# Attention followed by a clustering block: where one running maximum, the evictions and three scores stand in the order of the work

## The chip, the core and the metric

The kernel runs on one core of one Trainium2 chip. The metric is the time of one execution on the device in microseconds (us), as a median over several runs. Beside it there is one profiled execution, from which every row below comes.

The engines are named as in the profile: PE is TensorE (matrix products; PEld is its weight load), DVE is VectorE, ACT is ScalarE, POOL is GpSimd, SP is SyncE, which here only issues DMAs. Each engine works through its own queue in order. Matrix products are written to PSUM; the kernel's three PSUM pools together hold eight banks of 512 float32 per partition.

## What is computed

The input x is (4, 256, 64, 64) in float32, four images of N = 4096 points with C = 256 channels. Layer 0 is attention over the points of an image, layer 1 a block of clustering, a two-layer perceptron and a pointwise convolution. Cut to what matters:

```
# layer 0, per image; xf is (256, 4096)
q = wq @ xf + bq                # 32 x 4096
k = wk @ xf + bk                # 32 x 4096
v = wv @ xf + bv                # 256 x 4096
attn = softmax(q.T @ k, over the keys)
x = gamma * (v @ attn.T) + x
# layer 1
y = x + ls1 * cluster(group_norm(x))              # four cluster centres per head and fold
y = y + ls2 * (w2 @ gelu(w1 @ group_norm(y) + b1) + b2)    # 256 -> 1024 -> 256
z = relu(batch_norm(y * dw_w))
out = relu(batch_norm(wpw @ z))
```

## The kernel before, in words

**Stages.** The images follow one another. For each there is attention (`weighting`), then the clustering (`cluster`), then the perceptron and the last convolution (`mlp`, "multilayer part" below). The order of all instructions is written out by hand. Work of the next image is put between: `fill(n)` issues its projections of k, q and v one by one, and `mlp` issues its first scores.

**Units.** In attention the 4096 queries are cut into 8 blocks of 512 (`nb`) and the 4096 keys into 8 groups of 512 (`g`). A unit u = 8 nb + g is one group for one block, so an image has 64 units. A unit's scores are made in two halves of 256 keys (`half(u, h)`): two products into one PSUM tile of two banks (`products`, L423), a copy of it to SBUF on ScalarE (`kept`, L436) and a running maximum over the keys on VectorE (`highest_of`, L447). When all 16 halves of a block are done, `fold` (L504) joins the two rows of maxima; `highest` then reduces over the partitions with transposes (L534 to L551), writes the row to DRAM and reads it back to all partitions; the copy `known` (L569) puts it into `hold`. For block 1 of each image, where there is no time for that route, `across` and `spread` do it with PE.

**Who is ahead of whom.** Scores are made up to 11 units ahead (`LEAD`), so while block nb is weighed, the scores of block nb + 1 are made, by a table `at[u, part]`. Some halves have `kept_only`: their maximum is not taken from the PSUM tile but later, from the copy in SBUF. Such maxima are put on a list, `held`, and `caught(1)` takes one from it. The same is done for the second half of a block's first group (`g == 0`), of which the first half is only remembered (`saved`).

**What a unit does.** `exps(u + 1)` subtracts the block's maximum (two subtractions on VectorE, L586) and takes exponentials on ScalarE (L590 to L592), one quarter of them into the second half of `hold`. `factors(u + 1)` makes the sums of quarters that a product of two by two quarters with seven multiplications needs: one on VectorE (L609, it reads `hold`) and up to five on POOL (L595). `weigh(u, av, part)` (L661) multiplies with the values and adds up in four PSUM banks, `av` 0 to 3, in the order of `ORDER`, for the last unit of an image that of `LAST`. After the last group of a block `evict` (L686, ScalarE) takes the banks out, and `combine` joins them.

**Buffers.** The pool `ps_s` has two tiles of two banks. Within attention `hold` lives in one of them, so that one remains for scores. `ps_a` and `ps_m` have two banks each and hold `av`. In SBUF 13 tiles of one pool, `spool`, hold the image, the next image's input, the kept scores (`slots`), and what the multilayer part works on.

**Multilayer part.** It has 8 blocks of 512 points (7 in the third image, whose last is done later), in each four steps j. At the table's places `at[nb, j]` it makes a whole unit's scores of the next image (`score`), whose maxima go to a list `maxima` that `rest()` takes from one at a time (L495). `nxt.sums` are 32 sums of value quarters on POOL that the next image needs. Ahead of it stands the second group norm (`group_norm`, L277 to L297), for which the statistics of all points must be complete.

**The beginning** (`alone`) is the only place where the scores of an image's first block are not made beside another image's work.

Of the kernel before, what the change touches and what calls it, by code (L numbers as in the profile page):

```python
# [30 lines left out]
LEAD, SLOTS = 11, 10  # L31

QW = NB // 2
B21, B11, B12, B22 = range(4)
# [2 lines left out]


ORDER = (1, 5), (2, 3), (7, 6), (4,)
LAST = (7, 6), (1, 5), (2, 3), (4,)

PC = [
    "gn1_w", "gn1_b", "gn2_w", "gn2_b", "ls1", "proj_b", "ls2", "mlp_b2",
# [11 lines left out]
def attention_then_cluster_block(  # L57
# [250 lines left out]
    def attention(b, xs, ys):  # L308
# [146 lines left out]
        def half(u, h, kept_only=False):  # L455

            nb, g = divmod(u, GRP)
            if h == 0:  # L460
                begun(u)
            sc = products(u, h)
            kept(u, h, sc)
            own_copy = slots[u][:, PAIR[h]].rearrange("p h r n -> p r h n")
            if g == 0 and h == 0:
                highest_of(nb, own_copy)
            elif g == 0 or kept_only:
                held.append(lambda: highest_of(nb, own_copy))
            else:
                return lambda: highest_of(nb, tiles(sc))  # L470
            return lambda: None
# [328 lines left out]
        def alone():  # L800

            roots()
            for i in range(3):
                v_pair(i)
            staged("first", (("k", 0), ("q", 0)))
            k_unit(0)
            q_block(0)
            q_block(1)
            for i in range(3, 8):
                v_pair(i)  # L810
            for g in range(4):
                for f in sums(g):
                    f()
            for u in range(GRP):
                if u == 0:
                    begun(0)
                    staged("second", (("k", 1), ("q", 1)))
                    rest = load_rest()
                for h in range(2):
                    half(u, h)()  # L820
                caught(1)
                if u < 6:
                    v_pair(u + GRP)
                if u > 1:
                    next(rest, None)
            fold(0)
            for g in range(4, GRP - 1):
                for f in sums(g):
                    f()
            tp = turned_over(0, ps_m.tile([P, 4, P], F32, tag="m", name=f"tt_{b}_0"))  # L830
            half(GRP, 0)
            v_pair(14)
            dgs["dg"] = across(0, "w2", tp)
            spread(0, dgs["dg"])
            v_pair(15)
            wf()
            half(GRP, 1)
            exps(0)
            factors(0)
            for f in sums(GRP - 1):  # L840
                f()

# [31 lines left out]
        def weighting(next_x, fill, early, begin):  # L874
# [25 lines left out]
            for u in range(units):  # L900
# [35 lines left out]
                if u in shifts:  # L936
                    shift(shifts[u])
                weigh(u, av, 0)
                if g == GRP - 1:
                    evict(nb, av, 0 if more else 1)  # L940
                if short:
                    two = ps_s.tile([P, 2, NB], F32, tag="s", name=f"tt_{b}_{nb + 1}")
                    tp = turned_over(nb + 1, two[:, 0].rearrange("p (j n) -> p j n", j=4))
# [2 lines left out]
                weigh(u, av, 1)  # L946
                if short:
                    dgs["dg"] = across(nb + 1, "w2", tp)
                if g == GRP - 1:
                    evict(nb, av, 2 if more else 0)  # L950
                    if not more:
                        for _ in combine(nb, nc.vector):
                            pass
                if u == units - 2:
                    back_one(NBLK - 2)
                maxima = due(u, 2)
                if more and nb and g == GRP - 2:
                    known(mb)
                if g + 1 < GRP or more:
                    factors(u + 1)  # L960
                if ripe:
                    next(peak)
                    mb = next(peak)
# [81 lines left out]
    def cluster(b, ys, stats, cells, rest, fill, gelu, nxt, maxima, turn):  # L1045
# [342 lines left out]
        nxt.q_block(0)  # L1388
        nxt.k_unit(0)
        fill(1)  # L1390
        copies = []
        nxt.score(0, copies, maxima)
        copies.pop()()
        return stats2


# [116 lines left out]
    def mlp(b, ys, stats2, fill, nxt, blocks, turned, maxima):  # L1513
# [307 lines left out]
        acc, todo, slots = None, iter(()), (0,) * 4  # L1821
        own = ahead = iter(())

        at = {(u, 3): u for u in range(1, 7)} | {(7, 2): 7}
        if blocks < NBLK:
            at |= {(6, 1): 6, (6, 2): 7}
            del at[6, 3]
        for nb in range(blocks):
            end = nb == blocks - 1
            for j in range(4):  # L1830
                if j > 1:
                    rest()
                if end and j == 3:

                    rest()
                    rest()
                pw = (lambda: last(nb - 1, True, nc.gpsimd)) if end and j == 2 else lambda: None
                hs = first(nb, j, todo, slots, pw)
                if nb == 0 and j == 0:
                    fill(N)  # L1840
                if j > 1 or end:
                    rest()
                if nxt and nb:
                    for _ in range(2 if j < 2 else 1):
                        if nxt.sums:
                            nxt.sums.pop(0)()
                if j == 0:
                    if nb:
                        rectify = finish(nb - 1, acc)
                    acc = [  # L1850
                        ps_a.tile([P, NB], F32, tag=f"a{c}", name=f"mo{c}_{b}_{nb}")
                        for c in range(KC)
                    ]
                    if not end:
                        acc += [
                            ps_m.tile([P, NB], F32, tag="m", name=f"mo{c}_{b}_{nb}")
                            for c in range(2, 4)
                        ]
                    elif nxt:

                        nc.sync.dma_start(
                            out=a21_s, in_=w2.rearrange("(k p) m -> p k m", p=P)[:, :h_n, P:]
                        )
                        nxt.q_block(1)
                elif j == 1:
                    assert not drips and not hooks
                    if nb:
                        rectify()
                    if not end:
                        ahead = norm(nb + 1, nc.gpsimd)  # L1870
                        if nb:
                            own = factors(nc.gpsimd, pairs[nb - 1][:, 1], pairs[nb - 1][:, 0])
                        else:
                            own = left_factors()
                elif j == 2 and nb and not end:
                    pointwise(nb - 1)
                scored = nxt and (nb, j) in at
                if scored:
                    copies = []
                    nxt.score(at[nb, j], copies, maxima)  # L1880
                    copies.pop()()
                if len(acc) == KC:
                    todo = second(nb, acc, hs, j)
                    slots = (2, 1, 0, 1) if scored else (0, 1, 1, 2)
                else:
                    todo = second_by_seven(nb, acc, hs, j, own, ahead)
                    slots = (0, 2, 2, 3)
                    if scored:
                        slots = (3, 1, 2, 1)
                    elif j == 2 and nb:  # L1890
                        slots = (3, 1, 0, 3)
# [22 lines left out]
            nxt.exps(0, lambda: less(pairs[blocks - 1], nc.vector))  # L1914
        last(blocks - 1, bool(nxt), nc.vector, bool(nxt))
        if nxt:
            nxt.half(GRP, 1)
            nxt.factors(0)
        if blocks < NBLK:
            return late_block(b, y, gab)  # L1920
# [117 lines left out]
```

## Time and profile before

| | us |
|---|---|
| Runs of the kernel: median of 3 | 3239.3 |
| lowest and highest | 3239.08 and 3241.08 |
| The profiled execution | 3239.87 |
| its span, first to last instruction | 3237.8 |

The span and the time of the same execution differ by 2.1 us, which lie around the instructions. The granted TensorE clock is 0.99 on average. The costliest groups of instructions that bear on what follows, from the profile's list (busy time, mean of one):

| group | engine | count | busy us | mean ns |
|---|---|---|---|---|
| L436 copy of a score half | ACT | 512 | 514.8 | 1011 |
| L586 subtraction | DVE | 512 | 598.6 | 1209 |
| L609 sum of quarters | DVE | 256 | 311.7 | 1218 |
| L423 score product | PE | 1024 | 394.4 | 470 |
| L592 exponential, the longest of three | ACT | 256 | 266.9 | 1042 |

How to read it: a row's idle time is that of its engine just before the instruction, with the instruction that ended it behind an arrow. In timelines the columns are start, duration, engine, line, operation, what is written and read, and the shape. The profile splits a float32 product into two matmul rows, so counts of rows are not counts of products.

### The profile page before, as it was taken

To read this page: it belongs to the slowest core of one execution; us is meant where nothing else is said; L and a number is where in the kernel's file an instruction comes from. 1 tells how busy PE (TensorE), PEld (TensorE's weight loads), DVE (VectorE), ACT (ScalarE), POOL (GpSimd) and SP (SyncE) were. 2 spreads that over 40 slices of the span, in tenths; PEclk is the share of its full clock that TensorE was granted. 3 is DMA by queue.
4 is the path that set the end of the run, shared out by engine and by line. 5 is a ranking of instruction groups with operands and counts; after the bars stand their busy time and mean duration, and the time that the engine had idled before them with its cause. 6 is when DMAs were issued, how large, how long until landed. Compare 5 with 4: busy or idle time off the path is not lost.

```text
span 3237.8 us, 41259 instructions
## 1 busy us (share of the span) xinstructions
PE 3068.9 (95%) x14210; PEld 2504.8 (77%) x14210; DVE 2502.2 (77%) x3569; ACT 1772.2 (55%) x2807; POOL 2323.0 (72%) x2223
## 2 busy tenths in 40 slices
PE   6999999999999999999999999999999999998999
PEld 4778887788678888778867888786877787875786
DVE  3888887667788888777778888777678888877665
ACT  4566654545556665444555666634556566654444
POOL 3888888378488888648748888855866888894563
PEclk9999999999999999999999999999999999999999
DMA  4122126100111122610011221341011112150000
GB/s 162 40 59 62 53 63 187 51 32 30 43 49 54 61 59 85 165 50 20 30 50 49 62 59 56 111 128 50 30 43 43 53 59 62 56 142 7 14 20 27
DMA packets 105873, 200.39 MB, mean 62 GB/s; under 512 B 14416, under 2 KB 30400, under 8 KB 104128
## 3 DMA queue, kind: packets, MB, share of 16 engines
q1 hardware_dynamic: 101856, 181.94, 17.8%
q0 software_dynamic: 2976, 14.70, 2.4%
q8 instruction: 113, 1.85, 0.2%
q10 hardware_dynamic: 832, 1.11, 0.1%
q14 instruction: 96, 0.79, 0.1%
HBM read 149.37 MB, written 48.34 MB: 61 GB/s over the span
## 4 chain that ended last, share of the span: by engine, by line
PE 54%; DVE 15%; POOL 13%; ACT 10%; issue 6%; DMA 2%; ACTq 0%; SPq 0%; POOLq 0%; DVEq 0%
PE av L661 16%; PE mo L1650 10%; PE hq L1733 5%; POOL acc L595 5%; DVE top L447 4%; DVE s L586 4%; PE sc L423 4%; PE hp L1733 3%; PE hr L1733 3%; POOL t L595 3%; PE fv L1224 3%; PE vp L378 3%; ACT s L436 2%; ACT s L592 2%; POOL s L595 2%
## 5 line engine op out<-in xcount | busy, mean ns | idle before, releaser
L436 ACT COPY s<-sc 128x1024 f32<-128x1024 f32 x512 | 514.8, 1011 | 470.3 <-PE sc L423 468.8
L586 DVE TENSOR_TENSOR s<-s,hold 128x1024 f32<-128x1024 f32 x512 | 598.6, 1209 | 8.3 <-PE hold L576 8.3
L595 POOL TENSOR_TENSOR s<-t,s 128x512 f32<-128x512 f32 x256 | 345.4, 1349 | 315.5 <-DVE t L609 243.4
L661 PE MATMUL av<-t,v 128*128 128x256 f32 x2048 | 532.0, 382 | 14.0 <-DVE t L609 12.6
L595 POOL TENSOR_TENSOR acc<-acc,t 128x512 f32<-128x512 f32 x416 | 541.9, 1323 | 0.0
L661 PE MATMUL av<-s,v 128*128 128x256 f32 x2048 | 530.5, 382 | 7.1 <-ACT t L686 5.0
L661 PE MATMUL av<-s,sum 128*128 128x256 f32 x2048 | 527.1, 380 | 9.8 <-POOL s L595 9.8
L609 DVE TENSOR_TENSOR t<-s,hold 128x1024 f32<-128x1024 f32 x256 | 311.7, 1218 | 217.3 <-ACT s L592 64.7
L423 PE MATMUL sc<-q,k 128*128 128x512 f32 x1024 | 394.4, 470 | 79.0 <-DVE top L447 61.2
L661 PEld LDWEIGHTS av<-t,v 128*128 128x128 f32 x2048 | 389.8, 191 | 77.4 <-DVE t L609 16.5
L661 PEld LDWEIGHTS av<-s,v 128*128 128x128 f32 x2048 | 390.2, 191 | 71.1 <-ACT t L686 6.5
L661 PEld LDWEIGHTS av<-s,sum 128*128 128x128 f32 x2048 | 389.0, 190 | 66.2 <-POOL s L595 13.4
L447 DVE TENSOR_TENSOR top<-sc,top 128x1024 f32<-128x1024 f32 x326 | 397.7, 1220 | 40.1 <-ACT s L436 36.7
L1688 ACT ACTIVATE hs<-hs,pv_s 128x256 f32<-128x256 f32 x496 | 233.7, 503 | 344.4 <-DVE hs L1724 343.9
L1650 PE MATMUL mo<-hs,w 128*128 128x256 f32 x1512 | 390.4, 382 | 0.0
L595 POOL TENSOR_TENSOR t<-s 128x512 f32<-128x512 f32 x256 | 332.7, 1300 | 47.0 <-PE av L661 33.7
L1650 PEld LDWEIGHTS mo<-hs,w 128*128 128x128 f32 x1512 | 281.0, 190 | 54.3 <-ACT hs L1688 6.2
L423 PEld LDWEIGHTS sc<-q,k 128*128 128x128 f32 x1024 | 175.9, 189 | 164.7 <-DVE top L447 109.4
L590 ACT ACTIVATE hold<-s 128x512 f32<-128x512 f32 x256 | 154.2, 602 | 266.1 <-DVE s L586 261.0
L592 ACT ACTIVATE s<-s 128x1024 f32<-128x1024 f32 x256 | 266.9, 1042 | 0.0
L661 PE MATMUL av<-t,sum 128*128 128x256 f32 x1024 | 262.5, 378 | 0.9 <-DVE t L609 0.9
L1724 DVE TENSOR_TENSOR hs<-hq,hs 128x256 f32<-128x256 f32 x496 | 198.6, 421 | 79.9 <-PE hq L1733 69.9
(296 smaller groups left out, 4881.2 us busy)
## 6 DMA issues: line engine op xcount, KB each, us to landing
k<-k SPq DMA_DIRECT2D x256, 256.0 KB, 2.7
x<-in_x SPq DMA_DIRECT2D x62, 512.0 KB, 6.9
out<-xn SPq DMA_DIRECT2D x62, 256.0 KB, 2.1
att<-t SPq DMA_DIRECT2D x56, 256.0 KB, 3.8
x<-att POOLq DMA_DIRECT2D x12, 1024.0 KB, 10.0
q<-q SPq DMA_DIRECT2D x32, 256.0 KB, 4.1
w<-in_w SPq DMA_DIRECT2D x8, 1024.0 KB, 11.6
rden<-row_rd SPq DMA_DIRECT2D x28, 256.0 KB, 3.7
```

The costliest lines, as they stand in the source:

```text
L423: nc.tensor.matmul(sc[:, r, :], k_s[:, (2 * h + r) * P : (2 * h + r + 1) * P], qs[u // GRP], start=True, stop=True,)
L436: nc.scalar.copy(slots[u][:, PAIR[h]].rearrange("p h r n -> p r h n"), tiles(sc))
L447: nc.vector.tensor_tensor(top, src, top if saved[nb] is None else saved[nb], ALU.max)
L586: nc.vector.tensor_tensor(sh, sh, mb.to_broadcast([P, 2, 2, QW]), ALU.subtract)
L592: nc.scalar.activation(s[:, PAIR[1]], s[:, PAIR[1]], AF.Exp)
L595: nc.gpsimd.tensor_tensor(out, x, y, op)
L609: nc.vector.tensor_tensor(t31[u], s[:, B11 : B22 + 1 : 2], b12.to_broadcast([P, 2, 2, QW]), ALU.add)
L661: nc.tensor.matmul(av[bank][:, half_ * QW : (half_ + 1) * QW], a[:, r], t[:, r], start=(g == 0 and r == 0 and i in (1, 7, 2, 4)), stop=(g ...
L1650: return nc.tensor.matmul(bank[:, half * HB : (half + 1) * HB], a[:, j], t, start=start, stop=stop)
L1688: nc.scalar.activation(src, src, AF.Gelu_apprx_tanh, bias=pvc("b1", P, j + 4 * (i > 1)))
L1724: nc.vector.tensor_tensor(dst, ps, term, ALU.add)
L1733: nc.tensor.matmul(out, w, x, start=True, stop=True)
```

## The change

The change has six parts.

1. The maximum of the second half of a block's first group is no longer put on `held`: unless `kept_only` is given, it is taken from the PSUM tile. The two calls of `half(GRP, 1)` outside `weighting` now give `kept_only`.
2. In the last unit of a block the evictions of banks 0 and 2 (in an image's last block 0 and 1) stand together behind the copy of the score half that `due(u, 2)` makes. `known` now follows `factors`. `LAST` begins with products 1 and 5.
3. Before the multilayer part three units of the next image are scored instead of one (`EARLY`); the table `at` there has no scores in blocks 1 and 4.
4. Sums of value quarters are taken one per step instead of two, two, one, one, and three per step in the last block.
5. In `alone` k and q of the second half of the points are projected by `halved` (a tile of `ps_m` each) instead of `staged` (one tile of `ps_s`).
6. In `alone` the first exponentials and sums stand ahead of three of four last value halves, of the score half (8, 1), and of `wf`.

```diff
+EARLY = 3
...
-LAST = (7, 6), (1, 5), (2, 3), (4,)
+LAST = (1, 5), (7, 6), (2, 3), (4,)
...
-            elif g == 0 or kept_only:
+            elif kept_only:
                 held.append(lambda: highest_of(nb, own_copy))
             else:
                 return lambda: highest_of(nb, tiles(sc))
...
-                    staged("second", (("k", 1), ("q", 1)))
+                    halved("k", 1)
+                    halved("q", 1)
                     rest = load_rest()
                 for h in range(2):
                     half(u, h)()
-                caught(1)
...
             half(GRP, 0)
-            v_pair(14)
+            v_half(28)
             dgs["dg"] = across(0, "w2", tp)
             spread(0, dgs["dg"])
-            v_pair(15)
-            wf()
-            half(GRP, 1)
             exps(0)
             factors(0)
+            v_half(29)
+            v_pair(15)
+            half(GRP, 1, True)
+            wf()
...
                 weigh(u, av, 0)
-                if g == GRP - 1:
-                    evict(nb, av, 0 if more else 1)
...
                 weigh(u, av, 1)
...
+                if u == units - 2:
+                    back_one(NBLK - 2)
+                maxima = due(u, 2)
                 if g == GRP - 1:
-                    evict(nb, av, 2 if more else 0)
+                    evict(nb, av, 0)
+                    evict(nb, av, 2 if more else 1)
                     if not more:
                         for _ in combine(nb, nc.vector):
                             pass
-                if u == units - 2:
-                    back_one(NBLK - 2)
-                maxima = due(u, 2)
+                if g + 1 < GRP or more:
+                    factors(u + 1)
                 if more and nb and g == GRP - 2:
                     known(mb)
-                if g + 1 < GRP or more:
-                    factors(u + 1)
...
-        copies = []
-        nxt.score(0, copies, maxima)
-        copies.pop()()
+        for u in range(EARLY):
+            copies = []
+            nxt.score(u, copies, maxima)
+            copies.pop()()
...
-        at = {(u, 3): u for u in range(1, 7)} | {(7, 2): 7}
+        at = {(2, 3): 3, (3, 3): 4, (5, 3): 5, (6, 3): 6, (7, 2): 7}
...
-                    for _ in range(2 if j < 2 else 1):
+                    for _ in range(3 if end else 1):
                         if nxt.sums:
                             nxt.sums.pop(0)()
...
-            nxt.half(GRP, 1)
+            nxt.half(GRP, 1, True)
```

## The prediction, made before the result was known

> **What bounds the kernel now.** I read the engines' shares first, then the waits of TensorE, then the timelines around the longest of them.
>
> ```profile
> PE 3068.9 (95%) x14210; PEld 2504.8 (77%) x14210; DVE 2502.2 (77%) x3569; ACT 1772.2 (55%) x2807; POOL 2323.0 (72%) x2223
> ...
> PE sc L423 <- DVE top L447: 61.2, 64, 3.1
> PE av L661 <- DVE t L609: 13.5, 11, 2.0
> PE gnm_gn L279 <- DVE mv_gn L277: 12.8, 3, 4.3
> ```
>
> TensorE is busy 3068.9 of 3237.8 us, and the change alters none of its matmuls: at most the idle 169 us can be won. The other three lines (the view of the waits: total, times, longest) shows that the largest share is a score product waiting for VectorE's running maximum. One block of the second image, in the timeline (start, duration, engine, line):
>
> ```profile
> 1051.52 2.08 DVE L447 TENSOR_TENSOR top<-s,top 128x1024 f32<-128x1024 f32 x1
> ...
> 1053.40 0.59 ACT L569 COPY hold<-mr 128x512 f32<-128x512 f32 x1
> ...
> 1054.09 1.22 DVE L609 TENSOR_TENSOR t<-s,hold 128x1024 f32<-128x1024 f32 x1 [0.49 <-ACT hold L569]
> 1055.23 1.22 DVE L447 TENSOR_TENSOR top<-sc,top 128x1024 f32<-128x1024 f32 x1
> ...
> 1056.50 0.72 PE L423 MATMUL sc<-q,k 128*128 128x512 f32 x2 [1.46 <-DVE top L447]
> ...
> 1060.81 1.24 ACT L686 ACTIVATE t<-av,pv_s 128x512 f32<-128x512 f32 x2
> 1061.94 1.00 ACT L436 COPY s<-sc 128x1024 f32<-128x1024 f32 x1
> 1062.98 1.22 DVE L447 TENSOR_TENSOR top<-sc,top 128x1024 f32<-128x1024 f32 x1 [0.77 <-ACT s L436]
> 1064.26 0.73 PE L423 MATMUL sc<-q,k 128*128 128x512 f32 x2 [0.53 <-DVE top L447]
> ```
>
> Only one score tile circulates, since `hold` keeps the other buffer of `ps_s`: product, copy (1.0), maximum (1.2), next product. Two places per block break the beat: in unit 6 the held maximum from SBUF (2.08) and the copy of the next block's maximum (`known`, L569) push back L609; in unit 7 two evictions (1.24) stand ahead of a copy.
>
> The start times of VectorE's first subtraction (L586) give the rhythm: 7.00 us in units 0 to 3, though TensorE alone would need 6.88 (3.83 + 3.05 between scores that do not wait). So **the loop VectorE subtraction, ScalarE exponentials, L609, maximum, subtraction sets the pace**, and TensorE follows. From the subtraction in unit 5 to that in the next block's unit 0 (1041.43 to 1064.12) it takes 6.63 + 8.31 + 7.76 = 22.70. Over the 20 blocks 1 to 5 these stretches sum to 460.9.
>
> **Blocks 1 to 5.** The maximum of the first key group's second half, of the block whose scores are being made, moves from unit 6 to the end of unit 5 and reads PSUM. Replay with this trace's durations: it runs 1048.06 to 1049.28, so unit 6's first product, due at 1047.72, waits until 1049.33, a new stall of 1.6. Subtractions 1049.2 to 1051.5 (before from 1048.06), maximum to 1052.7, exponentials (2.10) to 1053.75, L609 to 1055.0 without waiting for `known`, second maximum to 1056.3, next subtraction 1056.2 (before 1056.37). In unit 7 exponentials end 1060.75, the copy now runs 1061.0 to 1062.0 ahead of the evictions, maximum to 1063.3, subtraction 1063.2 (before 1064.12). That is 21.8; I take 22.0 (up to 22.1 if queueing costs 0.3). `known` now waits for L609, which ends 1055.0; behind it on ScalarE is the copy of 1057.3, so 0.6 fits. The evictions end near 1064.5; bank 0 is due after 1064.7, bank 2 later: free. Where the row's DMA landed late, `known` ended 12.5 to 14.2 after unit 5's subtraction, and the next user now comes at 14.8: covered. 20 x 22.0 = 440, plus 2 for two stretches that hold matmuls of 1.9 instead of 1.03 us: **460.9 - 442 = 19 gained** (17 to 23).
>
> A rule against this: the Trainium skill, "PSUM — Partial Sum Buffer", section on bank collisions, says that two engines may not even read the same bank quadrant together, so copy and maximum must follow each other. The row agrees (the maximum waits for ACT s L436, 0.77), and it means that the new maximum holds the only tile. By the rule alone each block loses the 1.6: 32 us. By the subtraction rows TensorE has 0.12 per unit to spare and the 1.46 + 0.53 it lost later go away, so the loop decides. In its favour: "SBUF — State Buffer", "Who interferes with whom": VectorE with two SBUF inputs blocks against GpSimd's reads.
>
> ```profile
> L447 DVE TENSOR_TENSOR top<-sc,top 128x1024 f32<-128x1024 f32 x326 | 397.7, 1220 | 40.1 <-ACT s L436 36.7
> L447 DVE TENSOR_TENSOR top<-s,top 128x1024 f32<-128x1024 f32 x80 | 133.7, 1671 | 1.6
> ```
>
> The mean 1671 mixes 1.2 and 2.1; in these blocks the trace has 2.08. By the mean I would save 0.45 each, by the instance 0.86; the instance is used.
>
> **Block 0.** The same maximum now fills 1.24 us in unit 6 that VectorE idled for `hold`; TensorE lost 0.37 after it. 4 x 0.4 = **1.6**.
>
> **Block 6** has no scores left. There L609 waited for `known`, itself behind a shift (L757):
>
> ```profile
> 1285.76 2.17 ACT L757 ACTIVATE x<-x,gbv 128x1024 f32<-128x1024 f32 x2
> ...
> 1287.84 0.57 ACT L569 COPY hold<-mr 128x512 f32<-128x512 f32 x1
> 1288.50 1.22 DVE L609 TENSOR_TENSOR t<-s,hold 128x1024 f32<-128x1024 f32 x1 [4.84 <-ACT hold L569]
> ```
>
> L609 could go at 1285.9, so TensorE's 1.99 at 1289.78 vanishes. But the subtraction still needs `known` (ends 1288.4): 1288.5 instead of 1289.64. The next shift and evict 0 follow that subtraction, and the next block's first product waits for evict 0 (1.66 before, 2.6 now). Net 1.1 per image, **4.4** (0 to 8).
>
> **Last unit.** Product 6 waited for POOL (1.78; 4.10 in the fourth image). Products 1 and 5, 1.7 us, now go before 7 and 6. But the denominator waits for POOL's rows (L1002, at 1350.1 and 1351.0), which do not move. What comes earlier is `combine` and `complete`, 0.7: projections at 1351.4 for 1352.11. In the fourth image about 2. **4.1** (2 to 6). Evict 0 then 1 end where 1 then 0 did.
>
> **Three scores ahead of the norm.**
>
> ```profile
> 1426.02 0.59 DVE L277 BATCH_NORM_AGGREGATE mv_gn<-st 128x2 f32<-128x96 f32 x1
> ...
> 1426.67 0.59 PE L279 MATMUL gnm_gn<-mv_gn,left 128*128 128x1 f32 x2 [4.25 <-DVE mv_gn L277]
> ```
>
> Four more halves go into this hole: the copies (1.0 each) set the pace, ScalarE is idle from 1423.5 to 1429.6, and k of score 2 is loaded once score 0's products are done (1422.4 + 2.7 to landing). The last product ends near 1427, 0.4 late. SyncE's next work, writing k at 1438.96, is not touched. In return blocks 1 and 4 of the multilayer part lose a score. Between the first products of blocks I read 29.29 with a score and 27.37 in the fourth image without: 1.92 x 2 - 0.4 = 3.4, plus some of the half clock granted around this hole (about 0.2). 3 x 3.6 = **10.8** (6 to 13). VectorE gets 8 maxima more before block 2 (0.68 to 0.78 each); it is busy 22.4 of 30 there: hidden. If not, up to 2.5 an image return. Sums of 0.73 us on POOL fall from 6 to 4 a block, 8 move to the last one, where POOL worked 1.3 of 28 us: nothing. Slots held longer leave no spare buffer at block 4; a wait there is an output's DMA, 2.1: nothing to 2 an image.
>
> **The beginning.** `halved` writes to `ps_m` instead of taking a score buffer, so the 2.52 that the second product waited for st_second (at 37.93) goes. Units 0 to 5 then take 3.4 each, two score halves and one value pair: unit 6 starts at 55.4 instead of 57.68. The last two units and the 3.18 before L509 are paced by the maxima and stay: 2.3 gained. After that, one value half instead of two stands before the matmul that spreads the maximum (71.05, its input ready at 68.7): 1.65. The exponentials no longer stand behind value, `wf` and score copies on ScalarE: they can start when the subtraction ends, 74.5 instead of 75.65: 1.1. TensorE fills the time with the work moved behind. 2.3 + 1.65 + 1.1 = **5** (3 to 7).
>
> **Sum:** 19 + 1.6 + 4.4 + 4.1 + 10.8 + 5 = 44.9. The profiled execution took 3239.9: 3195.0. The median of the runs lies 0.6 below it, within what can be told.
>
> **Rivals.**
> - *Half of it* (0.25): the unscored blocks 1 and 4 do not shorten because VectorE takes the maxima there, and queueing eats the replay down to 0.3 a block. For it: 22.4 of 30 busy. Against: TensorE is full there, 30.0 of 30. Blocks 20 x 0.3 + 5 for late rows = 11, norm 0, rest 13 of its 15: 24, so 3216.
> - *The PSUM tile decides* (0.08): unit 6's product stalls 1.6 in 20 blocks and the 1.46 and 0.53 stay. Price 32; norm, beginning, block 6 and the end give back 24: 3248, slower. It decides from a stretch above 22.70 + 24/20 = 23.9. Against it: subtractions, not TensorE, keep the 7.00.
> - *It does not do what it says* (0.04): L609 depends on `known` in either order, and the evictions waited anyway: with the rest hidden, 3239.
>
> Forecast 0.60, own range 3184 to 3206; 0.03 lies below. Faster by over 0.2% (about what a measurement can tell): 0.60 + 0.25 + 0.03 = 0.88; same 0.04; slower 0.08. The range 3180 to 3222 leaves out the two last rivals and the half case's tail.
>
> **What would show it.** L447 top<-s,top falls by 24 of its 80 and top<-sc,top rises by as many. The stall of 1.46 appears one unit earlier as about 1.6, the 0.53 is gone; stretches of 22.0. The wait of gnm for mv falls from 12.8 to under 2. L609 no longer waits for hold L569. Blocks 1 and 4 take 27.4. I am wrong if the stretches stay at 22.7, or the idle time of sc <- top L447 (61) does not fall below 50.

## The result, and the profile after

| | before | after |
|---|---|---|
| median of the runs (four of each), us | 3240.19 | **3187.53** |
| lowest and highest, us | 3239.08 and 3242.06 | 3184.64 and 3195.52 |
| profiled execution and its span, us | 3239.87, 3237.8 | 3184.64, 3182.5 |

The ratio of the times is 0.984 (95% interval 0.982 to 0.986): faster by 1.6%. The forecast was 3195.0 with a range of 3180 to 3222. One run of the study is left out of the figures: of the four with one score ahead, one took 15501 us, and why is not known. The lines below number the changed kernel: those of before are shifted by 3, from about L1700 on by 5.

The first part of the page after, and the groups of the running maximum by their operands (count, shortest, median and longest in ns, first and last start):

```profile
PE 3049.3 (96%) x14210; PEld 2501.5 (79%) x14210; DVE 2489.0 (78%) x3569; ACT 1770.9 (56%) x2807; POOL 2315.4 (73%) x2223
```

```profile
L450 DVE TENSOR_TENSOR top<-sc,top x350: 1205/1223/1226, 38.0 to 2791.3; 128x1024 f32<-128x1024 f32 x175
...
L450 DVE TENSOR_TENSOR top<-s,top x56: 1205/1368/2299, 84.8 to 2501.4; 128x1024 f32<-128x1024 f32 x56
```

TensorE has the same 14210 matmuls, but it is busy 19.6 us less: its clock was halved for 47.8 us of this execution and for 64.9 before. The maxima from PSUM rise from 326 to 350 and those from SBUF fall from 80 to 56: 24 each way. The view of TensorE's waits (total, times, longest):

```profile
PE sc L426 <- DVE top L450: 38.8, 41, 1.5
PE av L664 <- ACT t L689: 10.9, 4, 2.7
PE den L1005 <- POOL rden L598: 10.2, 8, 2.5
...
PE av L664 <- DVE t L612: 3.8, 4, 1.0
...
PE gnm_gn L282 <- DVE mv_gn L280: 1.0, 3, 0.4
```

The wait for the maximum falls from 61.2 to 38.8, for L612 (L609 before) from 13.5 to 3.8, for the norm's statistics from 12.8 to 1.0. Others grew: that of the denominators for POOL, before 3.3 in six places, and that of the products for the evictions (`ACT t`), before 5.0 in three. The products' wait for POOL's sums `s` fell from 9.8 to 2.4.

**A steady block.** The timeline of the block of the second image that the prediction showed, now at 1019 us:

```profile
1026.17 1.17 DVE L450 TENSOR_TENSOR top<-sc,s 128x1024 f32<-128x1024 f32 x1
1027.27 2.33 DVE L589 TENSOR_TENSOR s<-s,hold 128x1024 f32<-128x1024 f32 x2
1027.39 0.73 PE L426 MATMUL sc<-q,k 128*128 128x512 f32 x2 [1.21 <-DVE top L450]
...
1031.88 1.22 DVE L612 TENSOR_TENSOR t<-s,hold 128x1024 f32<-128x1024 f32 x1 [1.15 <-issue]
...
1033.13 0.59 ACT L572 COPY hold<-mr 128x512 f32<-128x512 f32 x1
...
1039.10 1.01 ACT L439 COPY s<-sc 128x1024 f32<-128x1024 f32 x1 [0.29 <-PE sc L426]
1040.01 2.21 ACT L689 ACTIVATE t<-av,pv_s 128x512 f32<-128x512 f32 x4
1040.14 1.22 DVE L450 TENSOR_TENSOR top<-sc,top 128x1024 f32<-128x1024 f32 x1
...
1041.42 0.73 PE L426 MATMUL sc<-q,k 128*128 128x512 f32 x2
```

The stall of a score product is there one unit earlier (1.21). L612 no longer waits for the copy `known` (L572), which follows it. The score copy goes ahead of the evictions, and the last product shows no wait, where it had 0.53.

**Where the time came from.** I cut both traces at the same instructions: the first subtraction (L586, now L589) of a unit, the denominators' last product, the group norms', and the second product of the multilayer part (why not the first is shown further down). The rows add up to the difference of the profiled executions:

| stage, all four images | change, us | forecast |
|---|---|---|
| start to the first subtraction, and the first eight units of image 0 | -2.7 and -1.4 | -5 |
| block 0's last unit and block 1's first five | -4.3 | -1.6 |
| blocks 1 to 5 (the 20 stretches alone: 460.9 to 434.9) | -26.9 | -19 |
| block 6 | -4.8 | -4.4 |
| block 7 to its last subtraction (-2.7 of it in image 0) | -3.2 | 0 |
| last unit, to the denominators and projections | +4.5 | -4.1 |
| second norm to the multilayer part | -4.1 | } |
| multilayer part to the next image | -12.2 | } -10.8 together |
| sum, before rounding | -55.2 | -44.9 |

Two of these rows need care. Of the -4.3 only 2.4 (0.6 in each image's block 0) comes back in every version that leaves these units as in the change; block 1's first five units differ by more than the rest between such versions. Block 7 and the last unit have to be taken together: before, they last 59.3 to 59.4 in each of the images 0 to 2, though the subtraction between them lies elsewhere by up to 2.1. Together they are +1.3.

### The profile page after: what moved, and what is told of

Its sections match the earlier page's. It is cut to its first block, busy times and chain, and to the rows that moved or that the text cites. A ratio compares the mean times of both kernels' runs of the same rounds, so it can differ in the third digit from the quotient of the medians.

```text
span 3182.5 us, 41287 instructions
## 1 busy us (share of the span) xinstructions
PE 3049.3 (96%) x14210; PEld 2501.5 (79%) x14210; DVE 2489.0 (78%) x3569; ACT 1770.9 (56%) x2807; POOL 2315.4 (73%) x2223
## 3 DMA queue, kind: packets, MB, share of 16 engines
q1 hardware_dynamic: 101856, 181.94, 18.1%
## 4 chain that ended last, share of the span: by engine, by line
PE 63%; DVE 14%; POOL 12%; ACT 6%; issue 4%; DMA 1%; SPq 0%; ACTq 0%; POOLq 0%; DVEq 0%
PE av L664 25%; PE mo L1655 9%; PE sc L426 5%; POOL acc L598 5%; PE hq L1738 5%; DVE top L450 3%; DVE s L589 3%; PE hp L1738 3%; PE hr L1738 3%; PE fv L1227 3%; POOL t L598 3%; PE vp L381 2%; ACT s L439 2%; DVE t L612 2%; POOL s L598 1%
## 5 line engine op out<-in xcount | busy, mean ns | idle before, releaser
L589 DVE TENSOR_TENSOR s<-s,hold 128x1024 f32<-128x1024 f32 x512 | 598.9, 1209 | 8.4 <-ACT hold L572 5.1
L612 DVE TENSOR_TENSOR t<-s,hold 128x1024 f32<-128x1024 f32 x256 | 311.7, 1218 | 217.9 <-POOL acc L598 83.2
L426 PE MATMUL sc<-q,k 128*128 128x512 f32 x1024 | 392.3, 467 | 59.7 <-DVE top L450 38.8
L450 DVE TENSOR_TENSOR top<-sc,top 128x1024 f32<-128x1024 f32 x350 | 426.6, 1219 | 27.0 <-ACT s L439 22.5
```

The lines of the kernel that those rows point to most:

```text
L426: nc.tensor.matmul(sc[:, r, :], k_s[:, (2 * h + r) * P : (2 * h + r + 1) * P], qs[u // GRP], start=True, stop=True,)
L450: nc.vector.tensor_tensor(top, src, top if saved[nb] is None else saved[nb], ALU.max)
L589: nc.vector.tensor_tensor(sh, sh, mb.to_broadcast([P, 2, 2, QW]), ALU.subtract)
L612: nc.vector.tensor_tensor(t31[u], s[:, B11 : B22 + 1 : 2], b12.to_broadcast([P, 2, 2, QW]), ALU.add)
```

## The experiments

Unless it is said otherwise, each is the changed kernel with one edit. "Stretch" is the time from the subtraction in unit 5 of a block to that in the next block's unit 0, split by units, and its sum over the 20 blocks 1 to 5:

| version | typical stretch | sum |
|---|---|---|
| before | 6.63 + 8.31 + 7.76 = 22.70 | 460.9 |
| the change | 7.72 + 7.00 + 7.01 = 21.73 | 434.9 |
| maximum from SBUF again | 6.62 + 7.72 + 7.01 = 21.35 | 430.8 |
| `known` ahead of the sums again | 7.72 + 8.67 + 7.02 = 23.41 | 468.4 |
| evictions ahead of the copy again | 7.72 + 7.00 + 7.76 = 22.48 | 449.6 |

### The parts of the attention blocks, one put back at a time

**The maximum from SBUF.**

```diff
-            elif kept_only:
+            elif kept_only or (g == 0 and nb):
```

> The changed kernel with only the maximum put back on the held list, from SBUF, in all blocks that are scored during attention. Theory (the loop from subtraction to subtraction decides, and the held maximum fills a time in which VectorE would wait for the exponentials): units 5, 6, 7 take 6.63 + 7.8 + 7.0 = 21.45 instead of 21.73, kernel 0 to 6 us shorter. Rival (the prediction's step: the maximum from SBUF costs 0.86 a block): 22.6, kernel 17 us longer.

Measured: 3188.2 (3186.9 to 3189.9), ratio 0.984 [0.983, 0.986], not to be told from the change. In the timeline of its blocks (start, duration, engine, line):

```profile
1089.84 2.07 DVE L450 TENSOR_TENSOR top<-s,top 128x1024 f32<-128x1024 f32 x1
...
1091.83 1.21 DVE L612 TENSOR_TENSOR t<-s,hold 128x1024 f32<-128x1024 f32 x1
...
1094.23 0.73 PE L426 MATMUL sc<-q,k 128*128 128x512 f32 x2 [0.88 <-DVE top L450]
```

The slow maximum (2.07) delays L612 and costs 0.72 in unit 6. But in unit 5 no maximum stands ahead of the subtraction in VectorE's queue (in the change it runs at 1026.17, the subtraction at 1027.27), and that unit gains 1.10. So the first part of the change loses 0.38 in a steady block. Put back, it loses elsewhere: the last unit of block 0 takes 8.02 again instead of 7.42.

**The copy of the next maximum ahead of the sums.**

```diff
+                if more and nb and g == GRP - 2:
+                    known(mb)
                 if g + 1 < GRP or more:
                     factors(u + 1)
-                if more and nb and g == GRP - 2:
-                    known(mb)
```

> The changed kernel with only the copy of the next block's maximum (known) put back ahead of the sums of quarters. Theory (L612 waits for known, which now stands behind the copy of a later score): units 5 to 7 take 23.5, 1.8 more, in 20 blocks, and 1.1 per image in block 6: about 40 us longer. Rival (its place is worth the 0.49 that the trace of before shows, and 1.1 in block 6): 10 + 4 = 14 us longer.

Measured: 3227.3 (3223.4 to 3230.0), ratio 0.996 [0.995, 0.998]. The timeline of one block:

```profile
1107.27 0.60 ACT L572 COPY hold<-mr 128x512 f32<-128x512 f32 x1
1107.95 1.22 DVE L612 TENSOR_TENSOR t<-s,hold 128x1024 f32<-128x1024 f32 x1 [2.95 <-issue]
...
1110.36 0.73 PE L426 MATMUL sc<-q,k 128*128 128x512 f32 x2 [1.45 <-DVE top L450]
```

L612 starts as `known` ends, after 2.95 idle, which the profile puts down to nothing; the product behind it stalls 1.45. This order is worth 1.68 per block, 33.5 in the 20 stretches, and 1.2 in each block 6. The stretch of 23.41 is *longer* than before's 22.70: the maximum from PSUM, with `known` where it was, would have made these blocks slower. Beside the maximum from SBUF the same order is worth less: unit 6 takes 8.31 before and 7.72 in the version above, 0.59, since there L612 follows the slow maximum in any case.

**The evictions ahead of the copy.**

```diff
                 weigh(u, av, 0)
+                if g == GRP - 1 and more:
+                    evict(nb, av, 0)
...
+                if g == GRP - 1 and more:
+                    evict(nb, av, 2)
                 maxima = due(u, 2)
                 if g == GRP - 1:
-                    evict(nb, av, 0)
-                    evict(nb, av, 2 if more else 1)
                     if not more:
+                        evict(nb, av, 0)
+                        evict(nb, av, 1)
```

> The changed kernel with only the evictions of banks 0 and 2 put back ahead of the score copy in unit 7 (not in an image's last block). Theory (in unit 7 the copy, then the maximum, then the next subtraction wait for them): unit 7 takes 7.76 instead of 7.0 in 24 blocks, 18 us longer. Rival (with the other waits gone the evictions fit beside): less than 5 us longer.

Measured: 3204.2 (3199.0 to 3205.3), ratio 0.989 [0.987, 0.990]. Unit 7 takes 7.76 again in each of the 20 stretches: 0.75 each, as before. In block 0 it is 0.36.

**Two variants of the maximum.** One keeps it in SBUF only for blocks 3 to 7, whose scores are made from block 1 on, so that block 0 stays as in the change:

```diff
-            elif kept_only:
+            elif kept_only or (g == 0 and nb > 2):
```

> The changed kernel with the held maximum from SBUF only for blocks 3 to 7, that is where it is made in unit 5 of blocks 1 to 5. Theory (the loop): units 5, 6, 7 take 6.62 + 7.72 + 7.0 = 21.35 as with all held, but block 0's last unit keeps what it won: 7 us shorter than the changed kernel, near 3180. Rival: what blocks 1 to 5 win is lost before block 2 again, as with all held: same time.

Measured: 3185.0 (3177.7 to 3190.2), ratio 0.983 [0.981, 0.985]. The stretches sum to 430.6, 4.3 less and not 7, since some are longer than 21.35, and block 0's last unit keeps its 7.41; the whole isn't clear of the change by itself. The other takes unit 5's maximum from PSUM ahead of the second step of the next block's maximum over the partitions (`peak`), after which its row is sent through DRAM:

```diff
                 if ripe:
+                    for f in maxima:
+                        f()
+                    maxima = []
                     next(peak)
                     mb = next(peak)
```

> The changed kernel with unit 5's maximum (from PSUM) ahead of the second step of the next block's maximum instead of behind it, so that it fills 0.36 us in which VectorE waits for ScalarE's small copies. Theory (the loop): unit 5 takes 7.36 instead of 7.72, 20 x 0.36 = 7 us shorter. Rival (the row comes back 1.2 us later from DRAM and known with it, so that unit 6 waits): no shorter, or longer where the row is late.

Measured: 3198.3 (3189.8 to 3204.0), ratio 0.986 [0.985, 0.988]. In images 1 and 2 the stretch is the shortest of all, 7.31 + 6.85 + 7.0 to 7.6; in images 0 and 3 the last step takes up to 10.6. The views of the waits name what came late, first of TensorE, then of ScalarE:

```profile
PE sc L426 <- DMA k<-k: 24.7, 24, 2.3
...
ACT hold L572 <- DMA mr<-row_mx: 5.9, 5, 1.4
```

After the change the first line stands at 8.4 in 8 places, and the second isn't there. SyncE issues the loads of `k` for the next units behind the row's way through DRAM. In block 1 of the first image the reading back of the row is issued 10.3 us after unit 5's subtraction instead of 8.1, `k` lands at 16.4 instead of 14.7, and unit 7's first score product waits 2.27 for it. A gain of 0.4 per block is worth nothing if the next inputs come later than that.

### The last unit of an image

```diff
-LAST = (1, 5), (7, 6), (2, 3), (4,)
+LAST = (7, 6), (1, 5), (2, 3), (4,)
...
+                if g == GRP - 1 and not more:
+                    evict(nb, av, 1)
...
-                    evict(nb, av, 2 if more else 1)
+                    if more:
+                        evict(nb, av, 2)
```

> The changed kernel with only the last unit of an image put back: products 7 and 6 before 1 and 5, bank 1 taken out after the first part. Theory (POOL's row sets the end, the new order only bundles TensorE's waiting into one gap of 2.5 us, behind which the clock is halved): from the last subtraction to the denominator's second product 19.6 to 19.9 us instead of 20.4, no half clock there, whole kernel 1 to 3 us shorter. Rival (the prediction's step: the new order brings combine forward and saves 0.7 per image): 21.1 or more, whole kernel 3 to 4 us longer.

Measured: 3188.0 (3186.5 to 3192.0), ratio 0.984 [0.983, 0.986]: no difference in the whole. The timelines of the second image's last unit, first before and then after:

```profile
1342.41 1.57 POOL L595 TENSOR_TENSOR s<-t,s 128x512 f32<-128x512 f32 x1
1344.03 1.13 PE L661 MATMUL av<-s,sum 128*128 128x256 f32 x4 [1.78 <-POOL s L595]
...
1349.27 1.65 POOL L595 TENSOR_TENSOR rden<-acc 128x256 f32<-128x256 f32 x2
1350.11 0.41 PE L1002 MATMUL den<-rden,ones 128*32 128x128 f32 x4 [0.63 <-POOL rden L595]
...
1352.11 1.99 PE L378 MATMUL vp<-wv_s,x 128*128 128x256 f32 x8 [0.72 <-DVE t L715]
```

```profile
1316.13 1.60 POOL L598 TENSOR_TENSOR s<-t,s 128x512 f32<-128x512 f32 x1
...
1317.79 1.13 PE L664 MATMUL av<-s,sum 128*128 128x256 f32 x4
...
1323.19 1.65 POOL L598 TENSOR_TENSOR rden<-acc 128x256 f32<-128x256 f32 x2
1324.03 0.41 PE L1005 MATMUL den<-rden,ones 128*32 128x128 f32 x4 [2.51 <-POOL rden L598]
...
1325.23 3.41 PE L381 MATMUL vp<-wv_s,x 128*128 128x256 f32 x8
```

POOL goes from its sum `s` to the end of `rden` in 8.51 before and in 8.71 after. TensorE's wait has only moved, from 1.78 ahead of product 6 to 2.51 ahead of the denominators. The wait of 0.72 for the last combination is gone, as forecast; but the projections behind the longer hole took 3.41 for the eight rows that took 1.99, at a granted clock of one half. Such a window stands at these denominators in each of the images 0 to 2 of all ten traces that have the new order with these denominators, and in none of the two that have the old: the longer hole costs the clock.

In this stage the old order does gain: from the last subtraction to the second row of denominators it takes 18.1 to 22.5, in all four images together 2.3 less than the change (19.7 to 21.4). But between versions that share the new order this sum goes from 77.9 to 83.0 (the change: 82.2), so that single profiles don't give the size.

So POOL's chain should be shortened. The next edit takes the last block's denominators by two accumulating small products straight from `acc`, and leaves out POOL's two additions there (1.65):

```diff
+            if nb == NBLK - 1:
+                rdens[nb] = work.tile([P, NB], F32, tag="rden", bufs=1, name=f"rden_{b}_{nb}")
+                own["acc"] = acc
+                return
...
-                    rdens[nb][:, j * P : (j + 1) * P],
-                    start=True,
-                    stop=True,
...
+                for i in range(2):
...
+                        own["acc"][:, 1 - j // 2, i, (j % 2) * P : (j % 2 + 1) * P],
+                        start=(i == 0),
+                        stop=(i == 1),
```

> The change, but the denominator of an image's last block is taken by two accumulating small products straight from the accumulated sums, so that POOL's last additions (1.65 us beside the waiting products) are left out there. Theory: POOL's row of sums decides when the last unit ends; the hole of 2.5 us ahead of the denominators goes, and the stretch from the last subtraction to the denominators falls from about 20.5 to 18.5 us in each of four images: 5 to 8 us shorter, 3180 to 3183. Rival: another chain (the exponentials, DVE's last combination) ends next and the gain is 2 us or less.

Measured: 3186.1 (3184.4 to 3187.3), ratio 0.983 [0.981, 0.984]. The denominators' wait falls from 10.2 to 5.0, and in the timeline they follow POOL's `acc` directly:

```profile
1323.42 1.32 POOL L598 TENSOR_TENSOR acc<-acc 128x512 f32<-128x512 f32 x1
...
1324.80 0.67 PE L1010 MATMUL den<-acc,ones 128*32 128x128 f32 x16 [1.66 <-POOL acc L598]
...
1326.40 3.03 PE L381 MATMUL vp<-wv_s,x 128*128 128x256 f32 x8 [0.93 <-DVE t L722]
```

Then the combination on DVE comes last again (0.93), as the rival said. From the last subtraction to the second row of denominators it is 17.9 to 22.0 instead of 19.7 to 21.4, 3.5 less in all four images together. That lies within the spread named above, and the whole is not clear of the change: the shorter wait is shown, what it is worth is not.

### The scores ahead of the norm, and the sums of value quarters

```diff
-EARLY = 3
+EARLY = 1
...
-        at = {(2, 3): 3, (3, 3): 4, (5, 3): 5, (6, 3): 6, (7, 2): 7}
+        at = {(u, 3): u for u in range(1, 7)} | {(7, 2): 7}
```

> The changed kernel with one score ahead of the norm instead of three, and the old table of scores in the multilayer part. Theory (two scores less in the multilayer part, and the hole of 4.25 us ahead of the norm brings the half clock with it): from the norm's first product to the first product of the multilayer part 6.3 us instead of 3.96, from there to the next image 236 instead of 233.1, in three images: 16 us longer. Rival (the prediction's step, without the clock): 3.6 an image, 11 us longer.

Three runs gave 3192.2, 3193.2 and 3195.9, ratio 0.985 [0.984, 0.987]. By the mark of the expectation, the first product of the multilayer part, the stage from the norm takes 5.9 to 6.6 again (after: 4.0), and the multilayer part 233.2, 233.4 and 207.4, as after (233.1, 233.1, 207.3). But the mark deceives. The second image's first two products, after the change and then with one score ahead:

```profile
1405.44 0.67 PE L1738 MATMUL hp<-xn,w 128*128 128x256 f32 x2 [0.43 <-ACT probe L274]
1406.86 0.67 PE L1738 MATMUL hp<-xn,w_abcd 128*128 128x256 f32 x2 [0.75 <-DVE xn L1619]
```

```profile
1413.31 0.65 PE L1738 MATMUL hp<-xn,w 128*128 128x256 f32 x2
1413.80 0.59 PE L1738 MATMUL hp<-xn,w_abcd 128*128 128x256 f32 x2
```

After the change TensorE is early for the first and then waits for VectorE: the second starts 1.42 later instead of 0.49. So from here on the second product is the mark:

| images 0, 1, 2 | norm to multilayer part | multilayer part |
|---|---|---|
| before | 7.00, 6.75, 6.52 | 235.5, 235.5, 209.7 |
| the change | 5.38, 5.38, 5.38 | 231.6, 231.7, 205.9 |
| one score ahead | 6.55, 7.05, 6.48 | 232.8, 232.9, 206.9 |
| the sums as before | 5.36, 6.05, 6.61 | 233.9, 233.9, 208.0 |
| one score ahead, with idle products | 5.48, 5.36, 5.48 | 232.8, 232.9, 206.8 |

In these three images the three scores win 3.9 us ahead of the multilayer part and 3.4 within it, 7.3 in all. But before, with its scores where this version has them, the multilayer part took another 8.2: four of its scored blocks take 28.55 here and took 29.29, each 0.74 more. So most of what shortened it is not that scores left it but part 4 of the change, the sums. That was tried by itself, with three scores ahead:

```diff
-                    for _ in range(3 if end else 1):
+                    for _ in range(2 if j < 2 else 1):
```

> The change with the multilayer blocks' sums as before (more of them split off as instructions of their own on POOL). Theory: the scored blocks of the multilayer part become 0.74 us longer again each, four or so per image in images 0 to 2 and none in image 3, so the stretch from the first product of the multilayer part to the next image grows from 233.1 to about 236 us and the whole by about 8 us, to about 3196. Rival (the prediction's own term, 'nothing'): the sums are hidden beside TensorE, and the whole stays within 2 us of the change, 3186 to 3190.

Measured: 3194.7 (3193.1 to 3195.1), ratio 0.985 [0.984, 0.987]. The medians lie 7 above the change, but the ratios overlap, so the stages have to decide: the multilayer part is longer by 2.3, 2.2 and 2.1. Of the stretches from one block's first product to the next's, three are longer by 0.72, 0.72 and 0.74 and a fourth by 0.38; the last, where no three sums a step stand any more, is shorter by 0.28. The timeline in the first of these, with the sums as before and then after:

```profile
662.54 1.26 POOL L598 TENSOR_TENSOR sum<-v 128x256 f32<-128x256 f32 x1
663.88 1.03 POOL L598 TENSOR_TENSOR sum<-v,sum 128x256 f32<-128x256 f32 x1
664.87 0.91 POOL L1618 TENSOR_TENSOR xn<-xn 128x256 f32<-128x256 f32 x1
...
669.39 0.30 PEld L1655 LDWEIGHTS mo<-hs,w 128*128 128x128 f32 x2 [0.40 <-POOL hs L1667]
...
670.55 0.30 PEld L1738 LDWEIGHTS hp_pw<-xn,w 128*128 128x128 f32 x2 [0.44 <-POOL xn L1619]
```

```profile
659.15 1.26 POOL L598 TENSOR_TENSOR v<-v 128x256 f32<-128x256 f32 x1
660.49 1.03 POOL L1618 TENSOR_TENSOR xn<-xn 128x256 f32<-128x256 f32 x1
```

The second sum (1.03) stands ahead of POOL's own work for the block, the `xn` and `hs` that TensorE takes next. TensorE's weight loads wait for them, 0.29, 0.40 and 0.44, where they don't wait after the change; each is too short to be seen in the list of long waits. POOL is busy 24.3 of 29.0 us in that block, 22.3 of 28.0 after.

What do the three scores win ahead of the multilayer part: is that work done earlier, or is it the clock? The next kernel has one score ahead, and four pairs of score products in the hole that nobody reads (so TensorE does more in all):

```diff
-EARLY = 3
+EARLY = 1
+DUMMY = 4
...
+        for _ in range(DUMMY):
+            nxt.idle_products()
```

> As the kernel with one early score, and four more pairs of score products in the hole ahead of the norm, whose results nobody reads (3.3 us of TensorE without copies). If the clock is what the hole costs: no half clock behind it, norm to multilayer part near 4 us, first product to the next image still 236: 7 us shorter than with one early score alone. If only moved work counts: 6.3 stays, no shorter than with one early score.

Measured: 3187.8 (3187.3 to 3189.3), ratio 0.984 [0.982, 0.985], as the change, though not clear of the version without them either. From the norm to the multilayer part it takes 5.48, 5.36 and 5.48, as with three scores, and in the multilayer part it is no shorter than with one. A window of half clock still stands behind the norm in two of the three images, but of 3.4 us, where one score ahead had 6.8, 10.2 and 6.8. The windows around the hole in the second image (length, busy time of each engine with its count, granted clock, DMA share, GB/s), before and after:

```profile
1421.00:1426.00 5.00, 0.73 (x2) 0.30 (x2) 4.99 (x9) 2.47 (x3) 4.92 (x5) 0.99 0.00 0
1426.00:1432.80 6.80, 6.13 (x18) 5.18 (x19) 3.46 (x12) 2.17 (x4) 3.59 (x3) 0.51 0.00 0
```

```profile
1396.30:1401.40 5.10, 3.36 (x10) 1.56 (x10) 5.07 (x9) 4.58 (x6) 5.02 (x5) 1.00 0.35 103
1401.40:1408.20 6.80, 5.54 (x26) 4.41 (x27) 4.34 (x15) 4.17 (x8) 3.07 (x3) 1.00 0.00 0
```

With 0.73 of 5.00 us of TensorE work in the hole, the next 6.8 us run at 0.51; with 3.36 of 5.10, at full clock. The idle products do no work and win 3.8 of the 3.9 us: ahead of the multilayer part it is the clock. The 3.4 within it are the scores that were moved.

The profile of the change was lucky in this. It has no half clock behind any of its three norms, but of the 33 such places in the eleven traces with three scores ahead, 12 have one, and there the stage takes 5.9 to 6.9.

### The beginning

```diff
-                    halved("k", 1)
-                    halved("q", 1)
+                    staged("second", (("k", 1), ("q", 1)))
...
-            v_half(28)
+            v_pair(14)
...
+            v_pair(15)
+            wf()
+            half(GRP, 1, True)
             exps(0)
             factors(0)
-            v_half(29)
-            v_pair(15)
-            half(GRP, 1, True)
-            wf()
```

> The change with only the order of the beginning put back as before. Theory: the first subtraction of the first image starts at about 72 us instead of 69.4, with another 1.4 us in the first eight units, so the whole is about 4 us longer, 3191 to 3193. Rival: the start is limited elsewhere and the time is within 2 us of the change.

Measured: 3193.0 (3191.5 to 3193.3), ratio 0.985 [0.983, 0.986]. The wait of 2.5 for `st_second` is back, and the first eight units of image 0 take 62.67, as before (62.64; after 61.25). The first subtraction starts at 70.3, within the 67.9 to 70.6 of the versions that have the new beginning. So 1.4 of this part is shown; the rest of the 4.1 isn't separated from what varies between executions.

### Both gains together

The denominators from `acc`, and the maximum from SBUF for blocks 3 to 7.

> The denominators taken from the accumulated sums in an image's last block, together with the maximum kept in SBUF only for the later blocks (3 to 7). Theory: both gains stand beside each other, as they lie in different units: 3176 to 3181. Rival: the earlier units' gain only makes POOL's row later, as in the version with the SBUF maximum everywhere, and the whole is that of the denominators alone.

Measured: **3177.7** (3174.9 to 3183.8), ratio to before 0.980 [0.979, 0.982], clear of the change's 0.984 [0.982, 0.986]. Its stretches sum to 428.8, 6.1 less than after; the last unit takes 18.1 to 18.6 in images 0 to 2 and 23.4 in the fourth, 3.6 less in all. It is the fastest version of this study. That the two gains add up is not shown: it is not clear of the version with the maximum alone (0.981 to 0.985) nor of that with the denominators alone (0.981 to 0.984), and the last unit's 3.6 lie within the spread of that stage.

## Why the prediction was right, and where not

- **The sum**: 52.7 us by the medians and 55.2 in the profile, for 44.9. The direction and the main term were right. That the sum came so near is partly luck: in the profile, blocks 0 to 5 gave 10.6 more than forecast and the three scores with the sums 5.5 more, block 7 and the last unit 5.4 less.
- **What bounds the kernel**: right. The loop from subtraction to subtraction set the pace, and both places that the prediction named gave way. That only idle time can be won was not right: of the 55.2, TensorE's busy time gave 19.6. The 17 us less at half clock account for some 8.5 of these (an estimate: half of the 17), the rest is open.
- **Blocks 1 to 5**: the replay gave 21.8 for a stretch, and 21.73 was measured. The 19 were mis-sized at 26.0 in two terms: 22.0 was taken instead of the 21.8 (20 x 0.27 = 5.4), and 2 us were set aside for late stretches, of which 0.3 came (434.9 less 20 x 21.73). Which edit earns it was put wrongly: 0.86 was put down to the maximum read from PSUM. The runs give -0.38 for it, 1.68 for the order of `known`, 0.75 for the evictions; they don't add up to 0.97, because the slow maximum covered part of what `known` cost: beside it that order is worth 0.59, and 0.59 + 0.75 - 0.38 is 0.96.
- **The rule on bank collisions** alone would have cost 32. The stall it announces is there (1.21 in each steady block, not 1.6), and the subtractions of units 6 and 7 still take 7.00; unit 5 lost 1.10, as the replay had it. The rows were the better guide.
- **Block 0 and block 6**: 0.6 instead of 0.4 (the row of block 0 above holds other units too), and 1.2 instead of 1.1 per image. The product that waits for evict 0 waits 2.7, as the 2.6 forecast.
- **The last unit**: 4.1 forecast; with block 7, +1.3 in the profiled execution. That the denominator waits for POOL's rows, "which do not move", was right, and so was the 0.7 of `combine`; what failed is that a longer hole in one place was taken to be free, where in images 0 to 2 the clock was halved at it. In all runs together the order made no difference either way.
- **Three scores ahead**: the hole closed as said (12.8 to 1.0), and 16.3 came for 10.8, but none of its terms had the right size. The step that compared "29.29 with a score and 27.37 in the fourth image without" mixed two things: blocks with a score also had six sums on POOL. With the new sums the two kinds differ by 1.0 (28.55 and 27.5), and part of this comes back in other blocks, why is open; so the moved scores gave 3.4 in three images where 10.2 was forecast. The sums, costed at "nothing" and at 0.73 each (some take 1.03 to 1.27), gave 8.2 by the one run and 6.6 by the other. The clock, costed at 0.2 an image, gave 1.3 (3.9 in three).
- **The beginning**: 4.1 of 5 in the profiled execution, 1.4 of it shown by the run.
- **Rivals**: with 434.9 for the stretches, and 27.5 for the blocks that lost a score, "Half of it" fell, and "The PSUM tile decides" too. The version with `known` first comes near the latter's 23.9 with 23.41, but for another reason: there L612 waits for `known`.

## What to carry to other kernels

Replay a steady loop with the durations of its own trace: that came within 0.1 us of a stretch, while attributing the gain to single edits failed, because one edit's stall covers another's; only putting each back alone told them apart. An engine with room on average (POOL, busy 22.3 of 28.0 us in such a block) still delays the critical one when an instruction is put ahead of work that is needed next; what counts is the order in its queue. When moving work to fill a hole, ask which chain ends the hole: if it does not get shorter, the wait moves on, and a longer one can cost the clock as well. And cut two traces only at an instruction that cannot start early and then be followed by a hole: here such a mark put 1.0 us of an image into the wrong stage.

## What the runs showed of the chip

TensorE was granted half the clock in windows of 3.41 us or a multiple, in every trace, 38 to 83 us in all. After the change they follow its holes, for instance one of 2.7 us at 1270 (the next two groups of four matmuls took 1.91 and 1.81 instead of 1.03) and one of 2.5 at 1324. This window ahead of the projections after the change:

```profile
1325.60:1329.00 3.40, 3.40 (x11) 2.78 (x10) 3.02 (x4) 0.32 (x1) 0.00 (x0) 0.51 0.00 0
```

The denominators' hole of 2.5 us has such a window in each of the images 0 to 2, in all ten traces with that hole. (The hole of 2.7 us stands in twelve traces, once per image.) The Trainium skill ("TensorE: Matmul & The Clock Gate", Part 1) gives the length of the window, and says that it runs freely of the kernel; the traces agree with both, as within one of them all windows start whole multiples of 3.413 us apart, and this grid lies differently from trace to trace. It puts the loss of clock behind a whole idle window; here holes of 2.5 us were enough each time in these images, and such of 2.7 us in 33 of 48 places. The other thing not expected is how far useless products went: four pairs of score products that nobody reads win as much ahead of the multilayer part as moving real work there. The medians are 3187.8 with them and 3193.2 without, with ratios that overlap.
